# A half spectrum with its real and imaginary parts worked out once each, in a two-layer FFT and scan kernel

## The chip, the cores and the metric

The kernel runs on one core of one Trainium2 chip. The metric is the device time in microseconds (us) of one execution, and smaller is better. All data are 32-bit floats.

## The reference, cut to what matters

The input `x` holds 8 images of 128 channels of 128 x 128. Two layers follow each other. Only the first is touched here, and of it only the branch called the gate.

```python
feat = gelu(batchnorm(conv2d(x, conv_w, padding=3, dilation=3)))   # 128 -> 64 channels
F2 = fft2(feat)                                                    # per channel, 128 x 128
# branch 1: attention among 8 channels of a head, worked out from F2
out_f = abs(ifft2(attention(F2)))
# branch 2: the gate
gr = F2.real
cg = gelu(batchnorm(conv1x1(gr, cg1_w) + cg1_b))                   # 64 -> 4 channels
cg = sigmoid(conv1x1(cg, cg2_w) + cg2_b)                           # 4 -> 64 channels
gate = abs(ifft2(cg * F2))
y = concatenate([out_f, gate], axis=1) + x                         # first layer's output
```

The second layer is a 3 x 3 convolution, a small state-space scan over 8 tokens at every pixel, a group norm and a residual.

`feat` is real, so its spectrum is known from 65 of its 128 columns: column 128 - k is the mirrored conjugate of column k. Columns 0 and 64 have no partner.

## The kernel before, in words

`layer0` (line 142) takes two images at a time, in four passes of the loop over `p` (line 194). In each pass three stages follow one another, and each opens its own pools of on-chip memory, so the next stage's tiles wait until the previous stage's memory is free:

1. The convolution (lines 200 to 255) makes `feat` with 64 channels of two images on 128 partitions, its transpose `fT` (row index by channel), and the 4-channel projection `mT` of the gate. A small softmax follows.
2. The attention output (lines 257 to 274) turns `feat` into the first 64 output channels.
3. The gate (lines 276 to 340) makes the other 64 output channels. It works on groups of four channels: 16 groups for each of two images, 32 groups in a pass and 128 in all.

The gate's Fourier transform is done with matrix multiplies. `spectrum` (line 282) takes four channels. One multiply per channel at line 288, with the transposed feature as the stationary operand (`src[:, :, j0 + i + k]`, which picks one channel out of 128 and so steps 512 bytes from element to element) and the constant `fwd` of 256 columns as the moving operand, transforms along the image's width. `fwd` holds the real and imaginary parts in the packed order below, and both again as they are wanted for the second tile. ScalarE copies the product to `fa` two channels at a time (line 289). Lines 292 to 295 then transform along the height with four multiplies of 512 columns, into two PSUM tiles: `ep`, which holds the real part of columns 0 to 64 and minus the imaginary part of columns 1 to 63, and `eq`, which holds the imaginary part of columns 0 to 64 and the real part of columns 1 to 63.

`spectrum` runs first on `mT`, once per image, and eight small Gelu activations per image at line 303 turn it into `hid`, four hidden channels of 128 columns. Here too columns 65 to 127 repeat columns 1 to 63. It then runs once for each of the 32 groups. Per group:

- The image rows `xg` are loaded (line 310, SyncE's queue).
- VectorE forms the second 1 x 1 convolution in `cg` one channel at a time: one `tensor_scalar` (line 315) and three `scalar_tensor_tensor` (line 319) of 128 columns each, 16 instructions.
- ScalarE applies the sigmoid (line 322), 512 columns.
- VectorE multiplies `ep` and `eq` by `cg` into `gp` (lines 325 and 326), 512 columns each.
- TensorE transforms back along the height with 8 multiplies of 128 columns into `zps` (lines 329 and 330), VectorE copies them to `z` (line 332), and TensorE transforms back along the width with 4 multiplies into `ops` (line 335).
- ScalarE takes the absolute value into `og` (line 337), GpSimd adds `xg` (line 338), and ScalarE's queue issues the store (line 339).

The pools give two buffers to each tile in SBUF, two each to `ps1`, `ep` and `eq` in PSUM, and one each to `zps` and `ops`. In this layer the order on each engine's queue is set by a scheduler, which interleaves the work of neighbouring groups; each queue then runs strictly in that order. The second layer (`layer1`, line 344) has an order written out by hand and is the same in both kernels.

Of the kernel before, what the change touches and what calls it, by code (L numbers as in the profile page):

```python
# [9 lines left out]
F32 = mybir.dt.float32  # L10
AF = mybir.ActivationFunctionType
ALU = mybir.AluOpType
# [4 lines left out]
P = 128  # L17
# [4 lines left out]
CD = 64  # L22
HD = 8
MID = 4
# [12 lines left out]
NF = W // 2 + 1  # L37


def _fields(widths):  # L40
    at, out = 0, {}
    for name, n in widths:
        out[name] = (at, n)
        at += n
    return out, at


C0, C0_N = _fields([
    ("ident", P), ("fwd", 2 * P), ("cos", P), ("sin", P), ("nsin", P), ("inv", P),
    ("eighth", P), ("mask", P), ("nmask", P),  # L50
])
C1, C1_N = _fields([
# [15 lines left out]
def _constants():  # L68

    i = np.arange(P)  # L70
    c0 = np.zeros((P, C0_N), np.float64)

    def put(c, fields, name, v):
        at, n = fields[name]
        c[:, at:at + n] = np.asarray(v, np.float64).reshape(P, n)

    ang = 2.0 * np.pi * ((i[:, None] * i[None, :]) % P) / P
    cos, sin = np.cos(ang), np.sin(ang)
    re, im = np.arange(NF), np.arange(1, NF - 1)

    sin[:, [0, NF - 1]] = 0.0
    sin[[0, NF - 1], :] = 0.0
    put(c0, C0, "ident", np.eye(P))
    put(c0, C0, "fwd", np.concatenate([cos[:, re], sin[:, im], -sin[:, re], cos[:, im]], 1))
    put(c0, C0, "cos", cos)
    put(c0, C0, "sin", sin)
    put(c0, C0, "nsin", -sin)
    twice = np.where((re == 0) | (re == NF - 1), 1.0, 2.0)
    put(c0, C0, "inv", np.concatenate([cos[re] * twice[:, None], 2.0 * sin[im]], 0) / HW)
    head = (i[:, None] // HD == i[None, :] // HD).astype(np.float64)  # L90
    put(c0, C0, "eighth", head / HD)
    put(c0, C0, "mask", head)
    put(c0, C0, "nmask", (head - 1.0) * KEEP)

    c1 = np.zeros((P, C1_N), np.float64)
    put(c1, C1, "ident", np.eye(P))

    k, col = i % DI, np.arange(P) % 8
    put(c1, C1, "spread", k[:, None] == col[None, :])
    put(c1, C1, "spread_u", k[:, None] == col[None, :] + 8)  # L100

    put(c1, C1, "gather", np.stack(
        [(i % 8)[:, None] * LP + l == np.arange(DI)[None, :] for l in range(LP)], 1))
    tok = i // G
    put(c1, C1, "taps", np.stack(
        [tok[:, None] - np.arange(L)[None, :] + KC - 1 == k for k in range(KC)], 1))
    put(c1, C1, "same4", (i % LP)[:, None] == np.arange(LP)[None, :])

    put(c1, C1, "ends", np.stack(
        [(i % 8 == 0)[:, None] & (i % LP == l)[None, :] for l in (0, LP - 1)], 1))  # L110
    put(c1, C1, "half", np.stack(
        [(i % LP)[:, None] + hf * LP == np.arange(L)[None, :] for hf in range(NH)], 1))
    put(c1, C1, "group", (i[:, None] // 32 == i[None, :] // 32) / 32.0)
    return c0.astype(np.float32), c1.astype(np.float32)
# [27 lines left out]
def layer0(ctx, tc, x, w0, c0, x1):  # L142
# [5 lines left out]

    nc = tc.nc
    B = x.shape[0]
    const = ctx.enter_context(tc.tile_pool(name="l0_const", bufs=1))
# [7 lines left out]
    def cf(name):  # L161
        at, n = C0[name]
        return ct[:, at:at + n]

    def wf(name):
        at, n = W0[name]
        return wt[:, at:at + n]
# [19 lines left out]
    bs, bt = bn(wf("bn1_g"), wf("bn1_v"), wf("bn1_m"), wf("bn1_b"), None, 1, "bn1")  # L187
    gs, gt = bn(wf("cgbn_g"), wf("cgbn_v"), wf("cgbn_m"), wf("cgbn_b"), wf("cg1_b"), MID, "cgbn")
    w2, b2 = wf("cg2_w"), wf("cg2_b")
    tau_hw = const.tile([P, 1], F32, name="tau_hw")  # L190
    nc.vector.tensor_scalar(tau_hw, wf("tau"), float(HW), None, ALU.mult)

    CH = 16
    for p in range(B // 2):
        feat = big.tile([P, H, W], F32, name="feat")
        fT = big.tile([P, H, P], F32, name="fT")
        mT = big.tile([P, H, 2 * MID], F32, name="mT")
# [78 lines left out]
        with tc.tile_pool(name="l0_ff", bufs=2) as ff, \  # L276
                tc.tile_pool(name="l0_hid", bufs=1) as hp, \
                tc.tile_pool(name="l0_p1", bufs=2, space=PSUM) as p1, \
                tc.tile_pool(name="l0_p2", bufs=2, space=PSUM) as p2, \
                tc.tile_pool(name="l0_p3", bufs=1, space=PSUM) as p3:  # L280

            def spectrum(src, j0):

                a = ff.tile([P, 4, 2, P], F32, name="fa")
                for i in range(0, 4, 2):
                    ps = p1.tile([P, 2, 2, P], F32, name="ps1")
                    for k in range(2):
                        nc.tensor.matmul(ps[:, k], src[:, :, j0 + i + k], cf("fwd"), start=True, stop=True)
                    nc.scalar.copy(a[:, i:i + 2], ps)
                ep = p2.tile([P, 4, P], F32, name="ep")  # L290
                eq = p2.tile([P, 4, P], F32, name="eq")
                nc.tensor.matmul(ep, cf("cos"), a[:, :, 0, :], start=True, stop=False)
                nc.tensor.matmul(ep, cf("sin"), a[:, :, 1, :], start=False, stop=True)
                nc.tensor.matmul(eq, cf("cos"), a[:, :, 1, :], start=True, stop=False)
                nc.tensor.matmul(eq, cf("nsin"), a[:, :, 0, :], start=False, stop=True)
                return ep, eq

            hid = hp.tile([P, 2, MID, P], F32, name="hid")
            for b in range(2):
                ep, eq = spectrum(mT, b * MID)  # L300
                for m in range(MID):
                    for ps, s in ((ep, slice(0, NF)), (eq, slice(NF, P))):
                        nc.scalar.activation(
                            hid[:, b, m, s], ps[:, m, s], AF.Gelu,
                            bias=gt[:, m:m + 1], scale=gs[:, m:m + 1],
                        )
            for b in range(2):
                for c in range(0, CD, 4):
                    xg = ff.tile([P, 4, W], F32, name="xg")
                    nc.sync.dma_start(  # L310
                        xg, x[2 * p + b, CD + c:CD + c + 4, :, :].rearrange("c h w -> h c w"))
                    cg = ff.tile([P, 4, P], F32, name="cg")
                    for i in range(4):
                        k = (c + i) * MID
                        nc.vector.tensor_scalar(
                            cg[:, i, :], hid[:, b, 0, :], w2[:, k:k + 1], b2[:, c + i:c + i + 1],
                            ALU.mult, ALU.add)
                        for m in range(1, MID):
                            nc.vector.scalar_tensor_tensor(
                                cg[:, i, :], hid[:, b, m, :], w2[:, k + m:k + m + 1], cg[:, i, :],  # L320
                                ALU.mult, ALU.add)
                    nc.scalar.activation(cg, cg, AF.Sigmoid)
                    ep, eq = spectrum(fT, b * CD + c)
                    gp = ff.tile([P, 2, 4, P], F32, name="gp")
                    nc.vector.tensor_mul(gp[:, 0], ep, cg)
                    nc.vector.tensor_mul(gp[:, 1], eq, cg)
                    zps = p3.tile([P, 4, P], F32, name="zps")
                    for i in range(4):
                        nc.tensor.matmul(zps[:, i, :], gp[:, 0, i, :], cf("cos"), start=True, stop=False)
                        nc.tensor.matmul(zps[:, i, :], gp[:, 1, i, :], cf("nsin"), start=False, stop=True)  # L330
                    z = ff.tile([P, 4, P], F32, name="z")
                    nc.vector.tensor_copy(z, zps)
                    ops = p3.tile([P, 4, W], F32, name="ops")
                    for i in range(4):
                        nc.tensor.matmul(ops[:, i, :], z[:, i, :], cf("inv"), start=True, stop=True)
                    og = ff.tile([P, 4, W], F32, name="og")
                    nc.scalar.activation(og, ops, AF.Abs)  # L337
                    nc.gpsimd.tensor_add(og, og, xg)  # L338
                    nc.scalar.dma_start(
                        x1[2 * p + b][CD + c:CD + c + 4, :, :].rearrange("c h w -> h c w"), og)  # L340
# [514 lines left out]
def network(tc, x, w0, w1, c0, c1, out):  # L855
    B = x.shape[0]
    with tc.tile_pool(name="dram", bufs=1, space=DRAM) as dram:
        x1 = [dram.tile([C, H, W], F32, name=f"x1_{b}") for b in range(B)]
        layer0(tc, x, w0, c0, x1)
        layer1(tc, x1, w1, c1, out)  # L860
# [73 lines left out]
```

## Time and profile before

| | value |
|---|---|
| median of three runs | 15799.73 us (15787.79 to 15808.99) |
| profiled execution | 15803.33 us, span 15801.5 us |
| mean granted TensorE clock | 0.986 |
| busy over the span | TensorE 95%, VectorE 82%, GpSimd 76%, ScalarE 51% |
| first layer | 0 to 2945 us |
| four gate stages in it | 463 to 741, 1197 to 1476, 1931 to 2210, 2666 to 2945 us |
| second layer | 2945 us to the end |

The profile is one execution taken by the hardware profiler. A group row gives the source line, the engine, the operation, the output and input tiles with their shapes, how many there were, the total busy time in us and the mean of one in ns, and behind the last bar how long the engine sat idle just before and what released it. PE is TensorE's multiply and PEld its weight load, which overlaps the multiply before it. One multiply of 32-bit data is two PE records with a weight load each, and two to four such records can share one row of the timeline. DVE is VectorE, ACT is ScalarE, POOL is GpSimd and SP is SyncE.

### The profile page before, as it was taken

Reading aid. Unit: us, or ns where it says so; the run is one execution under the profiler, and the core shown is the slowest. Engines: PE = TensorE matmul, PEld = TensorE weight load, DVE = VectorE, ACT = ScalarE, POOL = GpSimd, SP = SyncE. Lnnn points to the kernel's source line nnn. Section 1 sums busy time; section 2 is a strip of 40 time slices with the busy share of each in tenths; the row PEclk is TensorE's granted clock in tenths of the full one; section 3 lists DMA queues with packets and bytes.
Section 4 is the critical chain, followed back from the end, with each engine's and each line's share of the span. In section 5 each row is a group of like instructions: output and inputs, shape, how many; then the busy total and the mean of one; then the engine's idle time right before and its main releaser. Section 6 shows DMA issues by size and latency. Waiting matters only on the chain.

```text
span 15801.5 us, 201588 instructions
## 1 busy us (share of the span) xinstructions
PE 15002.4 (95%) x71848; PEld 5732.8 (36%) x71848; DVE 12932.0 (82%) x13691; ACT 8126.9 (51%) x8726; POOL 12028.2 (76%) x5892
## 2 busy tenths in 40 slices
PE   9899898999999999999999999999999999999996
PEld 4546464533333333333333333333333333333332
DVE  0515142799999999999999999999999999999995
ACT  1312222455555555555555555555555555555553
POOL 0101101499989999999999999999999999999996
PEclk9999999999999999999999999999999999999996
DMA  2322222466666666666666666666666666666665
GB/s 73 90 78 75 75 75 77 93 120 119 119 120 136 136 135 134 136 135 135 133 135 135 136 133 135 135 135 133 135 135 136 133 135 135 135 133 135 136 135 135
DMA packets 1075755, 1932.60 MB, mean 122 GB/s; under 512 B 123968, under 2 KB 255040, under 8 KB 1058368
## 3 DMA queue, kind: packets, MB, share of 16 engines
q1 hardware_dynamic: 1001472, 1850.17, 54.9%
q10 hardware_dynamic: 73280, 69.54, 1.6%
q8 instruction: 571, 9.36, 0.2%
q14 instruction: 432, 3.54, 0.1%
HBM read 375.71 MB, written 201.33 MB: 37 GB/s over the span
## 4 chain that ended last, share of the span: by engine, by line
PE 71%; DVE 17%; issue 5%; ACT 4%; DMA 2%; POOL 1%; SPq 0%; ACTq 0%; DVEq 0%; POOLq 0%
PE da L554 18%; PE yps L620 8%; PE ups L554 7%; PE pm L134 7%; PE cps L134 6%; DVE da L585 6%; DVE h L593 4%; DVE h L569 4%; PE yps L626 3%; PE pm L506 3%; PE pm L639 3%; PE pm L518 3%; DVE hc L604 2%; PE da L499 2%; PE yps L610 2%
## 5 line engine op out<-in xcount | busy, mean ns | idle before, releaser
L599 POOL TENSOR_TENSOR hc<-h,cc 128x1024 f32<-128x1024 f32 x3584 | 8367.8, 2363 | 428.4 <-DVE h L593 414.3
L559 ACT ACTIVATE da<-da 128x1024 f32<-128x1024 f32 x3584 | 3618.7, 1010 | 4192.9 <-PE ups L554 2500.8
L569 DVE TENSOR_TENSOR h<-ups,bb 128x1024 f32<-128x1024 f32 x3584 | 4364.3, 1218 | 688.1 <-PE ups L554 307.2
L554 PE MATMUL da<-du,m_a 16*128 16x512 f32 x14336 | 4070.9, 644 | 139.1 <-DVE hc L604 134.6
L554 PE MATMUL ups<-du,m_u 16*128 16x512 f32 x14336 | 4117.5, 643 | 1.9 <-DVE h L569 1.3
L593 DVE TENSOR_TENSOR h<-da,h 128x1024 f32<-128x1024 f32 x2304 | 2821.1, 1224 | 79.1
L585 DVE TENSOR_TENSOR da<-da,h 128x1024 f32<-128x1024 f32 x2304 | 2819.1, 1224 | 4.7 <-issue 1.1
L134 PE MATMUL pm<-xin,l_wt 128*128 128x508 f32 (+1 forms) x4608 | 2409.4, 623 | 176.0 <-ACT xr L644 170.2
L591 POOL TENSOR_TENSOR h<-ah,h 128x1024 f32<-128x1024 f32 x768 | 1816.2, 2365 | 445.4 <-DVE ah L583 402.4
L554 PEld LDWEIGHTS da<-du,m_a 16*128 16x128 f32 x14336 | 1080.2, 184 | 2623.3 <-issue 1010.3
L620 PE MATMUL yps<-hc,l_ct 128*32 128x512 f32 x14336 | 1928.3, 610 | 0.0
L272 POOL TENSOR_TENSOR xr<-xr,sq 128x512 f32<-128x512 f32 x128 | 160.5, 1266 | 1652.5 <-ACT sq L271 1601.5
L134 PEld LDWEIGHTS pm<-xin,l_wt 128*128 128x128 f32 x4608 | 750.5, 189 | 1617.3 <-issue 1392.3
L554 PEld LDWEIGHTS ups<-du,m_u 16*128 16x128 f32 x14336 | 1125.3, 184 | 378.9 <-DVE h L569 297.2
L134 PE MATMUL cps<-xin,l_wt 128*64 128x500 f32 (+2 forms) x4608 | 1026.2, 584 | 39.2 <-issue 30.7
L222 DVE COPY fT<-tps 128x512 f32<-128x512 f32 x128 | 88.5, 692 | 1182.1 <-PE tps L221 1182.1
L559 ACT ACT_TABLE_LOAD x774 | 993.0, 1283 | 30.1 <-PE ups L554 1.4
L583 DVE TENSOR_TENSOR ah<-da,h 128x1024 f32<-128x1024 f32 x768 | 931.9, 1213 | 0.0
L338 POOL TENSOR_TENSOR og<-og,xg 128x512 f32<-128x512 f32 x128 | 164.4, 1284 | 968.5 <-ACT og L337 831.6
L620 PEld LDWEIGHTS yps<-hc,l_ct 128*32 128x32 f32 x14336 | 283.7, 108 | 1375.7 <-issue 970.9
L513 POOL TENSOR_TENSOR u<-dt,xc 128x512 f32<-128x512 f32 x512 | 652.7, 1275 | 169.8 <-ACT dt L508 169.8
L218 ACT ACTIVATE feat<-cps,bn_t,bn_s 128x512 f32<-128x512 f32 x128 | 99.5, 778 | 1224.1 <-PE cps L134 1224.1
(150 smaller groups left out, 16168.5 us busy)
## 6 DMA issues: line engine op xcount, KB each, us to landing
bb<-bc SPq DMA_DIRECT2D x2048, 256.0 KB
cc<-bc SPq DMA_DIRECT2D x2048, 256.0 KB
du<-dt SPq DMA_DIRECT2D x2048, 64.0 KB
du<-u SPq DMA_DIRECT2D x2048, 64.0 KB
xin<-x SPq DMA_DIRECT2D x112, 640.0 KB
xin<-x SPq DMA_DIRECT2D x48, 1408.0 KB
gn<-xr SPq DMA_DIRECT2D x256, 256.0 KB
v<-gn SPq DMA_DIRECT2D x256, 256.0 KB
```

Of the source, the lines that this page charges most:

```text
L134: nc.tensor.matmul(out[:, a:b, wa:wb], wt[:, t, :], src[:, r + dy + a - base:r + dy + b - base, wa + dx:wb + dx], start=(n == 0), stop=(n ...
L506: nc.tensor.matmul(ps, m_dtf, d["xc"][:, hf, :], start=True, stop=True)
L513: nc.gpsimd.tensor_mul(d["u", hf], d["dt", hf], d["xc"][:, hf, :])
L554: nc.tensor.matmul(o, w, v, start=True, stop=True)
L559: nc.scalar.activation(da, da, AF.Exp)
L569: nc.vector.tensor_mul(h, d["ups", s], state_row(i, "bb", s // GP))
L583: nc.vector.tensor_mul(d["ah"], da, before)
L585: nc.vector.tensor_mul(da, da, before)
L591: nc.gpsimd.tensor_add(h, d["ah"], h)
L593: nc.vector.tensor_add(h, d["da", s], h)
L599: nc.gpsimd.tensor_mul(hc, d["h", s], state_row(i, "cc", t))
L620: nc.tensor.matmul(d["yps"][g * DI:(g + 1) * DI], gather[:, t % LP, :], d["hc", GP * t + g // GP][:, g % GP], start=False, stop=(t in (3, ...
```

## The change

`fwd` shrinks from 256 to 128 columns: the cosines of columns 0 to 64, then minus the sines of columns 1 to 63. `spectrum` multiplies once per channel by it, copies all four channels in one ScalarE instruction, and works out the real part `er` and the imaginary part `ei` at 65 columns each. For each of the two, one multiply covers 4 x 65 = 260 columns and a second adds 4 x 63 = 252 columns into the middle of the same tile. `hid` and `cg` have 65 columns. The first term of the second 1 x 1 convolution moves to four ScalarE activations (Identity with a scale and a bias), and each further term is one product and one sum over four channels at once, with both factors broadcast. Four products now fill `gp` in the layout it had, with a sign in the last. The lines from `zps` on are unchanged.

```diff
-    put(c0, C0, "fwd", np.concatenate([cos[:, re], sin[:, im], -sin[:, re], cos[:, im]], 1))
+    put(c0, C0, "fwd", np.concatenate([cos[:, re], -sin[:, im]], 1))
...
+    w2r = w2.rearrange("p (c m) -> p c m", m=MID)
...
-                a = ff.tile([P, 4, 2, P], F32, name="fa")
-                for i in range(0, 4, 2):
-                    ps = p1.tile([P, 2, 2, P], F32, name="ps1")
-                    for k in range(2):
-                        nc.tensor.matmul(ps[:, k], src[:, :, j0 + i + k], cf("fwd"), start=True, stop=True)
-                    nc.scalar.copy(a[:, i:i + 2], ps)
-                ep = p2.tile([P, 4, P], F32, name="ep")
-                eq = p2.tile([P, 4, P], F32, name="eq")
-                nc.tensor.matmul(ep, cf("cos"), a[:, :, 0, :], start=True, stop=False)
-                nc.tensor.matmul(ep, cf("sin"), a[:, :, 1, :], start=False, stop=True)
-                nc.tensor.matmul(eq, cf("cos"), a[:, :, 1, :], start=True, stop=False)
-                nc.tensor.matmul(eq, cf("nsin"), a[:, :, 0, :], start=False, stop=True)
-                return ep, eq
+                a = ff.tile([P, 4, P], F32, name="fa")
+                ps = p1.tile([P, 4, P], F32, name="ps1")
+                for k in range(4):
+                    nc.tensor.matmul(ps[:, k], src[:, :, j0 + k], cf("fwd"), start=True, stop=True)
+                nc.scalar.copy(a, ps)
+                out = []
+                for name, of_re, of_im in (("er", "cos", "sin"), ("ei", "nsin", "cos")):
+                    e = p2.tile([P, 4, NF], F32, name=name)
+                    nc.tensor.matmul(
+                        e, cf(of_re), a[:, :, 0:NF], start=True, stop=False, skip_group_check=True)
+                    nc.tensor.matmul(
+                        e[:, :, 1:NF - 1], cf(of_im), a[:, :, NF:P], start=False, stop=True,
+                        skip_group_check=True)
+                    out.append(e)
+                return out
...
-                    for ps, s in ((ep, slice(0, NF)), (eq, slice(NF, P))):
-                        nc.scalar.activation(
-                            hid[:, b, m, s], ps[:, m, s], AF.Gelu,
-                            bias=gt[:, m:m + 1], scale=gs[:, m:m + 1],
-                        )
+                    nc.scalar.activation(
+                        hid[:, b, m, :], er[:, m, :], AF.Gelu, bias=gt[:, m:m + 1], scale=gs[:, m:m + 1])
...
-                    cg = ff.tile([P, 4, P], F32, name="cg")
+                    cg = ff.tile([P, 4, NF], F32, name="cg")
                     for i in range(4):
                         k = (c + i) * MID
-                        nc.vector.tensor_scalar(
-                            cg[:, i, :], hid[:, b, 0, :], w2[:, k:k + 1], b2[:, c + i:c + i + 1],
-                            ALU.mult, ALU.add)
-                        for m in range(1, MID):
-                            nc.vector.scalar_tensor_tensor(
-                                cg[:, i, :], hid[:, b, m, :], w2[:, k + m:k + m + 1], cg[:, i, :],
-                                ALU.mult, ALU.add)
+                        nc.scalar.activation(
+                            cg[:, i, :], hid[:, b, 0, :], AF.Identity, bias=b2[:, c + i:c + i + 1],
+                            scale=w2[:, k:k + 1])
+                    for m in range(1, MID):
+                        t = ff.tile([P, 4, NF], F32, name="cgt")
+                        nc.vector.tensor_mul(
+                            t, hid[:, b, m:m + 1, :].broadcast_to([P, 4, NF]),
+                            w2r[:, c:c + 4, m:m + 1].broadcast_to([P, 4, NF]))
+                        nc.vector.tensor_add(cg, cg, t)
                     nc.scalar.activation(cg, cg, AF.Sigmoid)
-                    ep, eq = spectrum(fT, b * CD + c)
+                    er, ei = spectrum(fT, b * CD + c)
+                    mid = slice(1, NF - 1)
                     gp = ff.tile([P, 2, 4, P], F32, name="gp")
-                    nc.vector.tensor_mul(gp[:, 0], ep, cg)
-                    nc.vector.tensor_mul(gp[:, 1], eq, cg)
+                    nc.vector.tensor_mul(gp[:, 0, :, 0:NF], er, cg)
+                    nc.vector.tensor_mul(gp[:, 1, :, NF:P], er[:, :, mid], cg[:, :, mid])
+                    nc.vector.tensor_mul(gp[:, 1, :, 0:NF], ei, cg)
+                    nc.vector.scalar_tensor_tensor(
+                        gp[:, 0, :, NF:P], ei[:, :, mid], -1.0, cg[:, :, mid], ALU.mult, ALU.mult)
```

More of the change, by code (lines that the diff above doesn't have):

```diff
@@ L48 @@
 C0, C0_N = _fields([
-    ("ident", P), ("fwd", 2 * P), ("cos", P), ("sin", P), ("nsin", P), ("inv", P),
+    ("ident", P), ("fwd", P), ("cos", P), ("sin", P), ("nsin", P), ("inv", P),
     ("eighth", P), ("mask", P), ("nmask", P),
@@ L292, in spectrum @@
[L292 to L295, printed above, removed]
-                return ep, eq
-            hid = hp.tile([P, 2, MID, P], F32, name="hid")
+                a = ff.tile([P, 4, P], F32, name="fa")
@@ L299, in layer0 @@
+                return out
+            hid = hp.tile([P, 2, MID, NF], F32, name="hid")
             for b in range(2):
-                ep, eq = spectrum(mT, b * MID)
+                er, _ = spectrum(mT, b * MID)
                 for m in range(MID):
-                    for ps, s in ((ep, slice(0, NF)), (eq, slice(NF, P))):
-                        nc.scalar.activation(
-                            hid[:, b, m, s], ps[:, m, s], AF.Gelu,
-                            bias=gt[:, m:m + 1], scale=gs[:, m:m + 1],
-                        )
+                    nc.scalar.activation(
+                        hid[:, b, m, :], er[:, m, :], AF.Gelu, bias=gt[:, m:m + 1], scale=gs[:, m:m + 1])
```

## The prediction

> **What bounds the kernel now.** I read the busy time by stage first, because the change touches only the gate, which runs in four stretches of the first layer.
>
> ```profile
> 463.00:741.00 278.00, 270.37 (x1304) 200.96 (x1304) 199.85 (x608) 88.32 (x152) 41.10 (x32) 0.98 0.21 60
> ...
> 2945.00:15801.00 12856.00, 12315.95 (x58912) 4206.14 (x58912) 11917.30 (x10899) 7448.41 (x7707) 11704.37 (x5633) 0.99 0.64 133
> ```
>
> The columns are the stretch, its length, then busy time of PE, PEld, DVE, ACT and POOL, the granted clock, the DMA share and GB/s. In the first gate stage TensorE is busy 270 of 278 us, VectorE 200, ScalarE 88, GpSimd 41. The second row, the second layer, has the same code in both kernels. The four gate stages last 278 + 279 + 279 + 279 = 1115 us, 7% of the span; this is all that can shrink.
>
> Next is the chain of waits inside one stage, from 600 to 620 us: nothing but multiplies.
>
> ```profile
> by line: PE ps L288 24.1%; PE ops L335 13.4%; PE ep L292 12.9%; PE ep L293 12.9%; PE zps L330 10.6%; PE zps L329 10.0%; PE eq L294 8.6%; PE eq L295 8.6%
> ...
> 600.23 0.22 PE zps L330 x2
> 600.45 1.42 PE ps L288 x6
> 601.87 0.89 PE ops L335 x8
> 602.76 0.86 PE ep L292 x2
> ```
>
> So TensorE's own pace sets the stage. By this chain a 512-column multiply costs 0.86 us (two records), a 128-column one 0.22, the four of `ops` 0.89. The 16 records of `ps` there take 1.42 + 0.99 + 1.43 = 3.84, or 0.24 each. A group costs 8 x 0.24 = 1.92 (`ps`), 4 x 0.86 = 3.44 (`ep`, `eq`), 8 x 0.22 = 1.76 (`zps`) and 0.89 (`ops`): 8.01 us. The timeline has `og` L337 at 563.37 and, nine groups later, at 635.74: 8.04 a group.
>
> The last reading is the weight loads, because it decides how much of the smaller `fwd` is worth anything.
>
> ```profile
> L288 PEld LDWEIGHTS ps<-l_ct,fT 128*128 128x128 f32 x1024 | 241.4, 303 | 6.8 <-ACT fa L289 5.3 <-issue 1.0
> L330 PEld LDWEIGHTS zps<-l_ct,gp 128*128 128x128 f32 x1024 | 165.4, 192 | 6.5 <-DVE gp L326 3.4
> ...
> 600.18 1.40 PEld L288 LDWEIGHTS ps<-l_ct,fT 128*128 128x128 f32 x6
> ```
>
> A load of one channel out of `fT` takes 303 ns where a contiguous one of the same size takes 192. Six run in 1.40 us, so they follow each other at (1.40 - 0.303) / 5 = 0.219 us. That is nearly the multiply's own 0.215 (from 1.42 for six against 0.99 for four), so it hides behind 256 columns today. It shows where a `ps` run follows a short multiply: the intercept of those two runs, 0.13 us, is about one load's excess over 0.11.
>
> [...] `zps` records follow at 0.11. [...] the 256 Identity activations at L473 indeed have no table load of their own row.
>
> **The change part by part, per group.** TensorE first.
> - `er` and `ei`: two multiplies of 260 and two of 252 columns take the place of four of 512. At 0.86 / 512 per column that is 2 x 0.437 + 2 x 0.423 = 1.72 instead of 3.44.
> - `ps`: still 8 records with 8 weight loads from `fT`, with 128 columns instead of 256. The multiply falls to 0.11, but the load stays at 0.219. So 8 x 0.219 = 1.75, less up to 0.11 at the end of a run where the last short multiply follows its load: 1.70 instead of 1.92. The bounds are 8 x 0.11 = 0.88, if the load hid after all, and 1.92.
> - `zps`, `ops`: unchanged, 2.65.
>
> The new group is 1.70 + 1.72 + 2.65 = 6.07. A pass has 34 spectra (32 groups and two on `mT`), so TensorE loses 34 x (5.36 - 3.42) = 66 us a pass, 264 in all. All of it lies on the path as long as TensorE stays the bound, so I check the others against 6.07.
>
> VectorE drops 16 instructions at L315 and L319 and two products of 512, together (152.9 + 428.2 + 88.5 + 88.5) / 128 = 5.92 us, and keeps `z` at 0.68. [...] Neighbouring records overlap: L319's 1536 records of 344 ns are busy for only 428 us, 100 less than end to end, and the 200 us busy per stage are 6.2 a group where the rows sum to 6.60. [...]
>
> ScalarE gains four Identity activations per group. The nearest row is the Gelu at L303, 128x65 with scale and bias by pointer, 0.41 each: at most 1.64. It loses one of two copies (0.588) and half the sigmoid's columns: 0.63 - 252 x 0.81 ns (the slope between 512 columns, 0.597, and 1024, 1.010) = 0.43. With copy 0.59, abs 0.60 and 0.47 for issuing the store it is 3.73. The store waits for GpSimd's 1.28, and the queue behind it with it, so 5.0: close, but below 6.07. That wait is old; what is new is what stands behind it. The Identity group is queued there, and VectorE's first sum waits for it, then the sigmoid, then `gp`, then `zps`. It costs nothing while `cg` is made a group or more ahead, which two `cg` buffers allow. I bound this added wait by 0 below and 0.4 us a group above.
>
> Ahead of the groups, the eight Gelus per image become four. The changed kernel's instructions hold two table loads per pass in the gate where the trace has four (8 at L303 and 8 at L322 over four passes). TensorE waited there once for 2.04 us behind them, so this is worth 0 to 2 us a pass; I take 0.5.
>
> GpSimd's sum and both DMAs (256 KB each) are unchanged, but come every 6.1 us: 524 KB / 6.1 us = 86 GB/s, share 0.21 x 8.04 / 6.1 = 0.28. The next `xg` is issued as soon as its buffer is free (SyncE's queue waited 245.6 us for L338 in the first stage), some two groups ahead, 12 us. That stays hidden. The constant `ct` is 64 KB smaller; it arrives beside the first conv and costs nothing.
>
> Sum: 15801.5 - 264 - 2 = 15535.5 against the profiled span. The three timed runs lie from 14 us below that span to 7 above, with the median 1.8 below it; I predict 15535.
>
> **Rivals.**
> - *The weight load hides.* If 128 columns halve `ps` to 0.88, 34 x 0.82 x 4 = 112 us more are saved: 15424. The pace of 0.219 and the 0.13 at the start of a run speak against it; that multiply and load have nearly one pace today, so that the trace can't fully part them, speaks for it.
> - *TensorE begins to wait or its writes get dear.* A 252-column product writes four runs of 63 into a tile with rows of 65; at twice its cost it would add 0.85 a group. Or the handshake between ScalarE and VectorE adds its 0.4. Between them 0.4 to 0.85 x 128 = 51 to 109 us are given back: 15586 to 15644. The shifted conv rows (128x500, 583 ns against 603 for 128x512) show no penalty for a cut-out window.
> - *VectorE becomes the bound: slower.* This decides once its ten instructions cost over (8.04 - 0.68) / 10 = 0.74 us each. The nearest row that could price them so is L270, 512 columns from SBUF beside a busy GpSimd, 0.774: then 10 x 0.774 + 0.68 = 8.42, 0.38 x 128 = 49 us slower, 15850. Half as many columns speak against it.
> - *Identity brings table loads.* With two a group (1.283 at L322) ScalarE needs 5.0 + 2.6 = 7.6: 15535 + 128 x 1.5 = 15730. L473 and those two loads a pass speak against it.
>
> **How the numbers follow.** The forecast has 0.68, the hidden weight load 0.13, the waits or dear writes 0.15, table loads 0.02, VectorE as bound 0.02. The range runs from 15424, the fast end of `ps`, to 15640, near the slow end of the second rival. About 0.2% (32 us) is what a measurement of this kernel can tell from no change; every case but VectorE's is beyond it on the fast side: faster 0.97, same 0.01 for a mixture, slower 0.02.
>
> **What would show it.** The gate stages should last 212 us instead of 279, with TensorE busy over 95% of them, VectorE near 150 and ScalarE near 110. Loads of `ps` should still take about 303 ns and follow at 0.22, and be the longest item of the chain per column. `er` should cost 0.43 a multiply and Identity about 0.4. The second layer should keep its 12856 us. The forecast is wrong if `ps` records follow at 0.11, if VectorE's waits for ScalarE's `cg` stand high among the waits with TensorE idle, or if the stages stay above 235 us.

## The result and the profile after

| | before | after |
|---|---|---|
| median | 15796.62 us (15787.79 to 15808.99, 4 runs) | 15540.6 us (15533.45 to 15541.24, 4 runs) |
| profiled span | 15801.5 us | 15539.1 us |
| the four gate stages, first `fa` copy to last store's issue | 277.3, 275.9, 276.3, 277.4 us | 211.9, 213.1, 211.9, 212.8 us |

The ratio is 0.9836, with a 95% interval of 0.9819 to 0.9853: 1.6% faster. The prediction was 15535 in a range from 15424 to 15640.

The profile after, busy time by stage, columns as in the prediction (stretch, length, then PE, PEld, DVE, ACT, POOL, clock, DMA share, GB/s):

```profile
460.50:672.50 212.00, 204.56 (x1296) 191.88 (x1296) 151.69 (x352) 97.89 (x236) 41.95 (x32) 0.99 0.28 79
...
2692.10:15539.10 12847.00, 12306.85 (x58912) 4204.80 (x58912) 11918.03 (x10899) 7448.53 (x7707) 11704.78 (x5632) 0.99 0.64 133
```

TensorE is still busy 96% of the gate stage, so it still sets it. VectorE is down by 48 us and ScalarE up by 10. The stages together lost 1106.9 - 849.7 = 257.2 of the 262.4 us by which the spans differ. The rest lies outside the gate: the second layer, whose code is the same, ran 8 us shorter in this execution, and the convolution and attention stages about 3 longer.

The costliest instructions of the changed gate, from the groups of the first layer (L336 is what was L329, L324 and L321 are VectorE's new sums and products, L316 the Identity):

```profile
L289 PEld LDWEIGHTS ps<-l_ct,fT 128*128 128x128 f32 x1024 | 233.4, 310 | 2.2
L289 PE MATMUL ps<-l_ct,fT 128*128 128x128 f32 x1024 | 233.3, 373 | 0.0
L336 PE MATMUL zps<-l_ct,gp 128*128 128x128 f32 x1024 | 198.4, 275 | 3.8 <-DVE gp L332 3.8
...
L324 DVE TENSOR_TENSOR cg<-cg,cgt 128x260 f32<-128x260 f32 x384 | 196.5, 513 | 111.9 <-ACT cg L316 110.4
L316 ACT ACTIVATE cg<-hid,l_wt 128x65 f32<-128x65 f32 x512 | 191.2, 431 | 66.1 <-DVE gp L332 36.6 <-DVE cg L324 24.4 <-POOL og L345 5.0
L321 DVE TENSOR_TENSOR cgt<-hid,l_wt 128x260 f32<-128x260 f32 x384 | 182.0, 503 | 50.9 <-DMA xg<-x 48.2
```

The first row is what the forecast turned on. Before, the `ps` multiplies had twice the columns:

```profile
L288 PE MATMUL ps<-l_ct,fT 128*128 128x256 f32 x1024 | 281.3, 404 | 4.1 <-ACT fa L289 4.1
```

Now they have half, yet a load still takes 310 ns and the busy time of `ps` is 233.3 us where it was 281.3. A `zps` multiply has the same 128 columns, and 1024 of its records keep TensorE busy for 198. The timeline shows the pace directly:

```profile
541.74 1.83 PEld L289 LDWEIGHTS ps<-l_ct,fT 128*128 128x128 f32 x8
541.85 1.91 PE L289 MATMUL ps<-l_ct,fT 128*128 128x128 f32 x8
...
543.59 1.06 PE L342 MATMUL ops<-l_ct,z 128*128 128x128 f32 x8
...
545.35 0.60 PE L294 MATMUL ei<-fa,l_ct 128*128 128x260 f32 x2
...
545.79 0.59 PE L296 MATMUL ei<-fa,l_ct 128*128 128x252 f32 x2
...
546.22 1.15 PE L289 MATMUL ps<-l_ct,fT 128*128 128x128 f32 x5
```

Eight loads in 1.83 us follow each other at (1.83 - 0.31) / 7 = 0.217 us, and the multiplies keep that pace: 1.74 us from the first `ps` to the first `ops`. The two multiplies of `ei` start 0.44 and 0.43 us before what follows them, half of the 0.86 of before. From these single runs the gain can be estimated by part. The second transform gives 136 x 4 x (0.86 - 0.43) = 234 us in 136 spectra, the first 136 x (1.92 - 1.74) = 24, together 258 where the stages lost 257.

Last, the waits of the first layer, with total us, times and the longest. The added one that the prediction named, VectorE's sums for ScalarE's Identity, is there: 110 us in all over four stages. It is VectorE's idle time and hardly TensorE's, which in this list waits on nobody in the gate for more than 23 us (on `fa`, four times, at the start of the stages).

```profile
DVE cg L324 <- ACT cg L316: 110.4, 76, 4.2
...
DVE z L339 <- PE zps L337: 85.4, 58, 2.2
ACT fa L290 <- PE ps L289: 82.4, 68, 2.3
```

### The profile page after: what moved, and what is told of

It is laid out like the page before. It is cut to its first block, busy times and chain, and to the rows that moved or that the text cites. A ratio compares the mean times of both kernels' runs of the same rounds, so it can differ in the third digit from the quotient of the medians.

```text
span 15539.1 us, 201046 instructions
## 1 busy us (share of the span) xinstructions
PE 14741.8 (95%) x71848; PEld 5706.0 (37%) x71848; DVE 12737.0 (82%) x12667; ACT 8165.2 (53%) x9062; POOL 12033.5 (77%) x5892
## 4 chain that ended last, share of the span: by engine, by line
PE 57%; DVE 17%; issue 4%; ACT 3%; DMA 1%; POOL 0%; SPq 0%; DVEq 0%; POOLq 0%; ACTq 0%
PE da L561 18%; PE yps L627 8%; PE ups L561 7%; PE pm L134 7%; DVE da L592 6%; DVE h L600 4%; DVE h L576 4%; PE yps L633 4%; PE pm L513 3%; PE pm L646 3%; PE pm L525 3%; DVE hc L611 2%; PE da L506 2%; PE yps L617 2%; ACT da L566 2%
```

## The experiments

The question was why 66 us a stage and not more: `fwd` was halved, and VectorE and ScalarE got less work per channel. My theory was that the spectrum alone made the gain, and that of its two halves the first transform gave little, because strided weight loads pace it. The rivals: the halved columns of `fwd` had paid; or VectorE's relief had.

Each run is set against the kernel before on the same chip. By its ratio of 0.9836 the changed kernel stands at 15538 to 15546 beside them. "Stage" is the first gate stage here, from the first copy to `fa` to the end of the last absolute value: 275.9 us before, 210.5 after. "Four stages" is the sum of all four, 1101.2 before and 844.0 after. It tells kernels that are close apart better than the median: the second layer, the same in all, lasts between 12846 and 12870 us in the traces, while the four stages of one trace agree within 1.7 us. It is read from one execution of each kernel.

**Undo the halving of `fwd` alone.**

```diff
-                ps = p1.tile([P, 4, P], F32, name="ps1")
-                for k in range(4):
-                    nc.tensor.matmul(ps[:, k], src[:, :, j0 + k], cf("fwd"), start=True, stop=True)
-                nc.scalar.copy(a, ps)
+                for i in range(0, 4, 2):
+                    ps = p1.tile([P, 2, 2, P], F32, name="ps1")
+                    for k in range(2):
+                        nc.tensor.matmul(ps[:, k], src[:, :, j0 + i + k], cf("fwd"), start=True, stop=True)
+                    nc.scalar.copy(a[:, i:i + 2], ps[:, :, 0])
```

> The changed kernel with 256 columns in the first transform again (the second half of the product is computed and not used; the copy takes the first half, two channels at a time as before). Theory, the weight loads pace the first transform: a load out of fT takes 0.22 us whether 128 or 256 columns follow, so only about 0.2 us a group comes back, 34 x 0.2 x 4 = 30 us: about 15570. Rival, the multiply's columns pace it: 0.82 us a group comes back, 112 us: about 15650.

Measured: 15579.0 us, ratio 0.9859 (0.9844 to 0.9874), stage 221.7, four stages 885.1. About 37 us come back (41 by the stages), near the 30 of the theory and not the 112 of the rival. The edit splits the copy to `fa` in two again, and what that costs is in the 37. In its groups the loads take 302 ns, much as they did, and the multiplies are only 25 us busier in all than with 128 columns:

```profile
L290 PE MATMUL ps<-l_ct,fT 128*128 128x256 f32 x1024 | 258.4, 388 | 0.0
L290 PEld LDWEIGHTS ps<-l_ct,fT 128*128 128x128 f32 x1024 | 238.8, 302 | 3.4
```

**Take the stride away.**

```diff
-        fT = big.tile([P, H, P], F32, name="fT")
+        fT = big.tile([P, P, H], F32, name="fT")
...
-                    nc.vector.tensor_copy(fT[:, r:r + 4, :], tps)
+                    nc.vector.tensor_copy(rows[:, r - r0:r - r0 + 4, :], tps)
+                    nc.vector.tensor_copy(fT[:, :, r:r + 4].rearrange("p c r -> p r c"), tps)
...
-                    nc.tensor.matmul(gram, fT[:, h, :], fT[:, h, :], start=(h == 0), stop=(h == H - 1))
+                    nc.tensor.matmul(gram, rows[:, j, :], rows[:, j, :], start=(h == 0), stop=(h == H - 1))
...
-                    nc.tensor.matmul(ps[:, k], src[:, :, j0 + k], cf("fwd"), start=True, stop=True)
+                    nc.tensor.matmul(ps[:, k], src[:, j0 + k, :], cf("fwd"), start=True, stop=True)
```

> The changed kernel with fT and mT stored channel by channel, so that the weights of the first transform are contiguous; VectorE makes a second, row-wise copy for the gram product in the convolution stage, where it has room. Theory: the loads fall from 310 to 192 ns, the first transform from 1.7 to 0.9 us a group, TensorE to 5.3; then VectorE (3 sums at 513, 3 products at 503, 4 products of gp, one copy: 5.4 us) is next, so a group takes 5.4 to 5.7: 50 to 85 us faster than the changed kernel, 15455 to 15490. Rival, the stride costs nothing: 15540 or slower.

Measured: 15516.84 us, ratio 0.9819 (0.9804 to 0.9833), stage 203.5, four stages 814.8. The cost of the stride to TensorE is shown; the time is not what I expected.

```profile
L291 PE MATMUL ps<-l_ct,fT 128*128 128x128 f32 x1024 | 133.0, 275 | 0.0
L226 DVE COPY fT<-tps 128x512 f32<-128x512 f32 x128 | 132.8, 1037 | 0.0
L291 PEld LDWEIGHTS ps<-l_ct,fT 128*128 128x128 f32 x1024 | 130.9, 192 | 4.4
```

Loads fall to 192 ns and `ps` from 233 to 133 us busy. The strided write on VectorE costs 1037 ns where the row-wise copy costs 692, but in the convolution stage it hides: the first copy to `fa` starts at 461.1 us, where it starts at 460.6 in the changed kernel. Of the 100 us taken from TensorE only some 26 reach the end (29 by the stages). Three waits of its first layer are about twice what the changed kernel has, or many times that (23.4, 3.8 and 14.7 us there):

```profile
ACT fa L292 <- POOL og L347: 49.1, 24, 2.2
...
PE zps L338 <- DVE gp L334: 35.8, 36, 1.4
...
PE ops L344 <- DVE z L341: 27.5, 45, 1.1
```

The copy to `fa` stands in ScalarE's queue behind a store that waits for GpSimd's sum (in one group the sum ends at 568.79, the store is issued at 568.82, and the copy starts at 569.33), and TensorE now waits for `gp` and `z`. So the gain had turned into a wait, and the next two questions were what part GpSimd plays, and by which road.

**Each part of the change alone.** First the gate part with the old spectrum. Its lines are the change's own, but for the products, which read the old tiles:

```diff
+                    nc.vector.tensor_mul(gp[:, 0, :, 0:NF], er[:, :, 0:NF], cg)
+                    nc.vector.tensor_mul(gp[:, 1, :, NF:P], ei[:, :, NF:P], cg[:, :, mid])
+                    nc.vector.tensor_mul(gp[:, 1, :, 0:NF], ei[:, :, 0:NF], cg)
+                    nc.vector.scalar_tensor_tensor(
+                        gp[:, 0, :, NF:P], er[:, :, NF:P], 1.0, cg[:, :, mid], ALU.mult, ALU.mult)
```

> The kernel before with only the gate part of the change: hid and cg at 65 columns, four channels at once, Identity on ScalarE, four products into gp; the spectrum stays at 256 and 4 x 512 columns. Theory, TensorE is the bound: VectorE falls by about 50 us a stage and the time does not move, 15797 within 20. Rival, VectorE's relief brings part of the gain: below 15750.

Measured: 15814.36 us, ratio 1.0007 (0.9999 to 1.0016), four stages 1107.4: no gain. VectorE fell from 200 to 141 us in the stage and TensorE stayed busy 274 of 278 (the columns are PE, PEld, DVE, ACT and POOL, as above):

```profile
463.00:741.00 278.00, 273.68 (x1304) 201.58 (x1304) 141.45 (x352) 121.48 (x269) 43.55 (x32) 0.99 0.21 60
```

Then the new spectrum with the second 1 x 1 convolution as it was, at 65 columns:

```diff
-                        nc.scalar.activation(
-                            cg[:, i, :], hid[:, b, 0, :], AF.Identity, bias=b2[:, c + i:c + i + 1],
-                            scale=w2[:, k:k + 1])
+                        nc.vector.tensor_scalar(
+                            cg[:, i, :], hid[:, b, 0, :], w2[:, k:k + 1], b2[:, c + i:c + i + 1],
+                            ALU.mult, ALU.add)
+                        for m in range(1, MID):
+                            nc.vector.scalar_tensor_tensor(
+                                cg[:, i, :], hid[:, b, m, :], w2[:, k + m:k + m + 1], cg[:, i, :],
+                                ALU.mult, ALU.add)
```

> The changed kernel with the gate's second 1x1 convolution on VectorE again, one channel at a time, 16 instructions of 65 columns. [...] Theory, TensorE bound and the gain is the spectrum's alone: 15540 if the instructions overlap as they did before. Rival, VectorE would have become the bound without the second part of the change: up to 0.7 us a group more, 15630.

Measured: 15539.74 us, ratio 0.9832 (0.9815 to 0.9848), four stages 829.3: the changed kernel's time. VectorE is busy 192 of the stretch of 212 us here, against 152 in the changed kernel, and is still not the bound:

```profile
460.50:672.50 212.00, 202.79 (x1296) 192.44 (x1296) 192.49 (x672) 56.53 (x108) 41.02 (x32) 0.98 0.28 80
```

The whole gain is the spectrum's. The stages are even 15 us shorter in all than the changed kernel's, too little for the medians to tell, so by this one trace of each the gate part gave a little of the gain back.

**GpSimd's sum left out, with contiguous weights.** The output lacks the residual in the gate's 64 channels.

```diff
-                    nc.gpsimd.tensor_add(og, og, xg)
```

> The kernel with contiguous weights, and GpSimd's sum of og and xg left out, so the gate's channels are stored without the residual. Contiguous weights alone took the first stage from 212 to 205 us where TensorE's work fell by 28. Theory, the rest is lost to GpSimd's sum: VectorE's two-operand SBUF instructions stretch while it runs (510 to 580 ns against 425) and ScalarE's queue stands behind the store that waits for it. Then the stage falls to 185 to 192 us and the time to 15430 to 15460. Rival, the losses are VectorE's and ScalarE's own order and the long way round from copy to gp: no change, about 15515.

Measured: 15449.22 us, ratio 0.978 (0.9765 to 0.9794), stage 186.1, four stages 745.6. GpSimd's sum is behind the loss. Without it VectorE's sums and products take 425 and 426 ns, where they took 514 and 577 with it. The store is still issued on ScalarE's queue, for 0.37 us each, so the time of the issue itself is not what was lost.

**TensorE's order by hand.** With strided weights, and then with contiguous ones (the same loop):

```diff
+            with tc.manual_schedule(engines={E.PE}):
+                for t in range(-1, ns + 2):
+                    for k in range(4):
+                        if 0 <= t + 1 < ns:
+                            first(t + 1, k)
+                        if 0 <= t < ns:
+                            second(t, k)
...
+                    if 2 <= t - 2 < ns:
+                        back_w(t - 2)
+                    if 2 <= t - 1 < ns:
+                        back_h(t - 1)
```

> The changed kernel with TensorE's order written out by hand in the gate: each multiply of the next group's first transform between the multiplies of this group's er and ei, then ops, then zps; weights still strided. Theory, a strided load hides behind the 0.21 us of an er record and is exposed only between the two records of a multiply: 0.11 x 4 = 0.43 us a group less, up to 58 us in all, 15485, if VectorE and ScalarE keep up; with their waits 15485 to 15525. Rival, the order of loads does not matter: 15540.

Measured: 15490.63 us, ratio 0.9806 (0.9791 to 0.982), stage 197.9, four stages 790.5. This is a second sign of the same cost: with the same loads from the same strided tile, some 48 us go when half of them, the first of each multiply's two, run beside a record of `er` or `ei`. The timeline shows such a multiply taking 0.32 us, from 561.99 to 562.31, where two records at 0.217 take 0.43:

```profile
561.77 0.52 PEld L294 LDWEIGHTS ps<-l_ct,fT 128*128 128x128 f32 x2
561.99 0.49 PE L294 MATMUL ps<-l_ct,fT 128*128 128x128 f32 x2
...
562.31 0.59 PE L308 MATMUL er<-fa,l_ct 128*128 128x252 f32 x2
```

> Contiguous weights and the hand-written TensorE order together. TensorE has 5.3 us a group. Theory, the order gives each gp, z and copy a fixed distance to its reader, so the group falls to 5.4 to 5.7: 15450 to 15490. Rival, VectorE and ScalarE set the pace whatever TensorE's order: 15515 as with contiguous weights alone.

Measured: 15491.5 us, ratio 0.9805 (0.9791 to 0.982), stage 194.5, four stages 777.3. It is faster than contiguous weights alone, and just outside what I expected. Against the order with strided weights the median is the same, and the first stage is 3.4 us shorter although TensorE has 14 us less to do in it (busy 180.7 against 194.7). So TensorE was no longer what held it. The two rows are this order with strided and with contiguous weights:

```profile
461.00:640.00 179.00, 177.40 (x1174) 172.05 (x1175) 138.94 (x329) 95.11 (x224) 38.88 (x27) 0.98 0.28 82
461.00:640.00 179.00, 168.38 (x1210) 156.35 (x1211) 140.61 (x337) 93.07 (x228) 40.31 (x28) 0.98 0.28 83
```

In the first stage with contiguous weights ScalarE's Identity waited 57 us for `gp` (to free `cg`) and VectorE's sums 32 for the Identity.

**The store on another queue.** The store of `og` goes to SyncE's queue, whose loads of `xg` wait for the same sum anyway (in the changed kernel's timeline a load and a store are both issued at 542.29, when a sum of 1.27 us from 540.99 has ended).

```diff
-                    nc.scalar.dma_start(
+                    nc.sync.dma_start(
                         x1[2 * p + b][CD + c:CD + c + 4, :, :].rearrange("c h w -> h c w"), og)
```

> Contiguous weights, and the store of og issued on SyncE's queue instead of ScalarE's, so that ScalarE does not stand behind GpSimd's sum. Theory, the held ScalarE queue delays the copy to fa (it waited for GpSimd 6 times for 12 us in the first stage) and the Identity group: 5 to 10 us a stage, 15475 to 15500. Rival, VectorE's stretched instructions are what is left: 15515.

Measured: 15452.6 us, ratio 0.9782 (0.9766 to 0.9799), stage 187.0, four stages 746.2, the fastest kernel of this study with the whole computation: 2.2% faster than before and some 86 us faster than the change. Against contiguous weights alone one instruction's queue brought some 60 us (0.9819 to 0.9782; 69 by the stages), more than I expected and about as much as leaving GpSimd's sum out. TensorE is busy 177.5 of the 179 us from 461 to 640, against 163.6 with contiguous weights alone, which is the first row here:

```profile
461.00:640.00 179.00, 163.57 (x1151) 148.81 (x1152) 140.86 (x318) 90.55 (x218) 36.07 (x27) 0.99 0.29 82
461.00:640.00 179.00, 177.50 (x1270) 164.23 (x1269) 141.59 (x349) 94.39 (x233) 39.42 (x30) 0.99 0.33 91
```

So the road is ScalarE's queue. VectorE's stretched instructions are still there, at 455 and 477 ns, and do not decide. What this run doesn't part is the hold itself from the new order that the scheduler finds once the store has moved.

**The same store with the weights strided**, the changed kernel with this edit alone.

> The changed kernel with the store of og on SyncE's queue and nothing else changed, so the weights are strided. Theory, with strided weights TensorE is the bound at 6.1 us a group and busy 204.6 of the stage's 212 us, so a freer ScalarE queue can bring at most the rest beside the start, 0 to 4 us a stage: 15525 to 15545. Rival, the store's place brought the 64 us between the two kernels with contiguous weights by itself: below 15490.

Measured: 15532.11 us, ratio 0.9826 (0.9811 to 0.984), stage 205.7, four stages 824.8. The interval overlaps the changed kernel's; the stages are 19 us shorter in all. The held queue costs little as long as the loads pace TensorE. By the stages the store alone brings 19 us and contiguous weights alone 29, but both together 98.

**The second convolution on VectorE, where TensorE is fast**: contiguous weights, the store on SyncE's queue, and the edit of the spectrum alone.

> Contiguous weights and the store on SyncE's queue, with the second 1x1 convolution on VectorE one channel at a time, as in the run with the spectrum alone. There VectorE was busy 192 us of the stage. Theory, with TensorE at 5.3 us a group VectorE's 6.0 becomes the bound, so the gate part of the change, which brought nothing by itself, is worth some 15 to 20 us a stage here: 15510 to 15540 instead of 15453. Rival, it brings nothing here either: 15453.

Measured: 15489.78 us, ratio 0.9802 (0.9785 to 0.9818), stage 197.3, four stages 789.5. VectorE is busy 177.3 of the 179 us from 461 to 640:

```profile
461.00:640.00 179.00, 172.68 (x1207) 154.59 (x1207) 177.26 (x638) 51.17 (x99) 36.89 (x29) 1.00 0.29 84
```

It is the bound, and the gate part of the change, worth nothing by itself, is worth some 32 to 37 us here by ratio and by median, and 43 by the stages. That is 10 to 11 a stage, where I had put down 15 to 20.

## Why the prediction was right, step by step

- **TensorE sets the stage, before and after.** Right: busy 97% of the first stage before, 96% after, and the gate part alone brought nothing.
- **`er` and `ei` at 0.43 a multiply.** Right: in the timeline of the changed kernel an `ei` starts at 545.35 and its second multiply at 545.79, 0.44 later. Runs of 63 columns in rows of 65 cost nothing that can be seen: the second multiply takes 0.43. So that side of the second rival falls.
- **`ps` held by its loads at 0.219, 1.70 a group.** Right in mechanism. The pace is 0.217, and the run of eight shown above takes 1.74 us, from 541.85 to the first `ops` at 543.59. The first rival, a hidden load, is refuted by the wide `fwd` (37 us back, not 112) and by contiguous weights (`ps` from 233 to 133 us). A load takes 310 ns strided and 192 contiguous; why the stride costs this, no run shows.
- **VectorE near 150 a stage.** Right on the whole: 151.7 us, or 151.7 / 32 = 4.74 a group. The figure was my estimate, and its parts came out unevenly. The products into `gp`, one of whose inputs is in PSUM, take 428, 423, 409 and 410 ns. The sums and products of `cg`, with both inputs in SBUF and much the same size, take 513 and 503, which I had not foreseen. Without GpSimd's sum (and with contiguous weights) they take 425 and 426. They take 425 and 425 also with the gate part alone, which keeps the sum; around 608 us in that run, GpSimd starts only while the last of them runs (at 607.92, that product at 607.73).
- **Identity below 0.41, ScalarE near 110 a stage.** The first was too low for a single one, 431 ns. But neighbours overlap: four of them keep ScalarE busy for 191.2 / 128 = 1.49 us a group, inside the 1.64. ScalarE is 98 in all, less than forecast. There is no table load at L316.
- **The added wait, 0 to 0.4 us a group.** It showed as VectorE's wait. Its cost is not measured by itself. By the traces the gate part as a whole costs 15 us of the four stages against the spectrum alone, 0.1 us a group, which is inside the bound.
- **The sum.** 264 + 2 were forecast for the gate and 257 came; another 5 came from outside the gate. That the median is within 6 us of the forecast is partly luck.

What the prediction didn't see, and didn't need, is the next bound. I named the store's hold of ScalarE's queue and called it old and hidden. At 6.1 us a group it was nearly hidden: moving the store brought 19 us by the stages. At 5.3 the same move brought 69.

## What to carry to other kernels

Halving a multiply's columns paid here only down to the pace of its weight loads: with strided loads a record of `ps` follows at 0.22 us, where with contiguous ones the same 128 columns follow at 0.11 (twelve records in 1.50 us). So read the weight loads' pace before counting columns, above all where the stationary operand is cut out of a tile with a stride (310 ns a load here, against 192). While TensorE was the bound, taking VectorE from 200 to 141 us a stage brought nothing; with contiguous weights and the store on SyncE's queue, the same part of the change was worth 10 to 11 us a stage. So run each part alone to see which one paid. A DMA that waits for another engine's result belongs on a queue where nothing urgent stands behind it: here the move brought 69 us by the stages with contiguous weights, and 19 with strided ones.

## What was not expected of the hardware

- VectorE instructions with two SBUF inputs, 425 ns in the run without GpSimd's sum, took up to 1.55 us beside a GpSimd sum in the changed kernel (541.00, with GpSimd busy from 540.99); those with one input in PSUM kept their time, 403 to 433 ns over all 512 of them.
- A VectorE copy from PSUM that writes single elements 512 bytes apart took 1037 ns for 512 columns, 1.5 times the contiguous 692.
- Moving one DMA issue of 0.46 us from ScalarE's queue to SyncE's brought some 60 us, 0.5 us a group, with contiguous weights, and 14 us, within the intervals, with strided ones (69 and 19 by the stages).
